# Idle matrix products in two pauses of the start, and the first tail's parts one step sooner, in an attention and ternary-FFN kernel on one core

## The chip, the core and the metric

The kernel runs on one core of one Trainium2 chip. The metric is device time in microseconds (us), the median of several runs of the whole kernel.

## What is computed

The input x has 8 batches of 1024 tokens with 256 features, all in f32. With `ln` for layer normalisation over the features:

```python
q, k, v = ln(x) @ Wq, ln(x) @ Wk, ln(x) @ Wv      # 16 query heads, 4 key/value heads, 16 wide
q, k = rope(q), rope(k)
o = softmax(q @ k.T / sqrt(256)) @ v               # each key head serves 4 query heads
x = x + ln(o @ Wo)
w = where(W > d, 1, where(W < -d, -1, 0)) * alpha  # d = 0.7 * mean(abs(W))
x = x + ln(ln(x) @ w.T + bias)
```

## The kernel before, in words

A **unit** is 512 tokens (half a batch); there are 16. A unit's attention has four **blocks** (one query head of each key group at a time), each block has 8 **steps** (key tiles of 128), and each step has four score tiles, so s counts score tiles from 0 to 2047 and step n ends at s = 4n + 4. One unit is 32 steps, 128 score tiles.

*Precision.* TensorE takes f32 operands as a high and a low part. `split_hi` (ACT, or POOL at L157) rounds a tile to its high part; `split_lo` (L162) subtracts that from the tile. `product` (L297, its matmuls recorded at L301) adds three products of the parts. So every projection needs both parts, turned by TensorE transposes (`transposed`, L262, matmuls at L267, copied out by ACT at L271).

*Project* (L323) makes a unit's q, k and v: normalise, split, `x` (the transposes), `q_product` (pq, L451), `kv` (pkv), `rotate_q` (L315 to L317), `rotate_k` (L400 to L406), `split_k`, `split_q`, and for the first unit `k` (ptk, L417) and `PickRows` (L531; pqs at L549, pk at L539), which places rows of q and k for the score products. *Tail* (L738) does what follows a unit's attention: `fetch`, `invert`, `scale` (the quotient), `attn` (pa, the product with Wo), `stats_a` (first norm and sum x1), `stats_x` (second norm, split), `x` (pt_ot), `ffn` (pf) and `stats_f` (last norm, sum, store). A tail works on two halves, 0 and 1, of its unit.

*The three products of attention.* `max_scores` (sm, L600) makes scores for the row maxima, which DVE reduces (mx, L612 and L625). `exp_one` (se, L673) makes them again, with the maximum taken off, for ACT's exponential (e, L694). `av_piece` (av, L714) multiplies by v.

*Order.* The kernel writes the order of PE, DVE, ACT and POOL by hand up to s = 8 (L1194), of PE, DVE and ACT behind that (L1250); POOL and the DMA queue of SP are then ordered when the kernel is compiled. The opening, in PE's order, is: eleven idle products (`keep_warm(11)`, L1197), the first unit's four groups of transposes (the loop at L1217: high and low part of its first half, then of its second), pq of half 0, pkv, the transposes ptv, pq of half 1, ptk, the picks, and the second unit's first transposes. Ten starting steps (-10 to -1) follow, in which DVE reduces four maxima each.

`keep_warm(n)` (L1002) issues n products of 128x512 of tiles that lie ready. They write a bank that nothing reads, so their only effect is TensorE's work.

From s = 0 the work goes in **windows** of 2 or 3 score tiles. Parts of projects and tails are entered in a list by step (`at`), step k of T_PARTS, T_FIRST, P_PARTS and the like counted from the unit's start. `collect` moves a step's parts to `ready`, and `do_parts` (L1127) takes them first in, first out. A part that needs a bank of PSUM (x, q, v, kv_and_dram, attn, ffn and others, `banked`, L1093) is taken in a window of two only, one to a window, and a part behind it waits. T_FIRST (L989) holds the steps of the first unit's tail, in the order of T_PARTS (L980), from step 32.

Of the kernel before, what the change touches and what calls it, by code (L numbers as in the profile page):

```python
# [28 lines left out]
def kernel(  # L29
# [120 lines left out]
    def fill_constant_parts(i):  # L150
        if i > 0:
            fill_rows(k_st[i], 1, NROW, 64 - NROW)
        nc.gpsimd.memset(v_aug[i], 1.0)
# [7 lines left out]
    def split_lo(eng, lo, src, hi):  # L161
        eng.tensor_tensor(lo, src, hi.bitcast(F32), ALU.subtract)  # L162
# [7 lines left out]
    def parts_of(w, name):  # L170
        return [const.tile(list(w.shape), F32R, name=name + l) for l in "hl"]

    def by_pairs(w):
        return w[:, :, :D].rearrange("p c (m e) -> p c e m", e=2)

    def by_place(w):
        return w[:, :, :D].rearrange("p c (e m) -> p c e m", e=2)
# [325 lines left out]
    def row_pickers():  # L503

        sel = q_st[1].rearrange("p j c t -> p (j c t)")[:, : 4 * G * P]
        nc.vector.memset(sel.bitcast(F32), 0.0)
        sel = sel.rearrange("p (l e j x) -> p l e j x", l=2, e=2, j=G)
        selk = tailp.tile([P, 2, P], F32R, tag="hl1", name="selk")
        nc.vector.memset(selk.bitcast(F32), 0.0)
        half = small.tile([P, P // 2], F32, tag="half", name="half", bufs=1)  # L510
        nc.vector.tensor_tensor(half, ident[:, : P // 2], ident[:, P // 2 :], ALU.add)
        eye = half.rearrange("p (a j d) -> p j a d", a=2, j=G)
        for e in range(2):
            for band, l in enumerate((0, 1, 0)):
                rows = sel[:, l, e].rearrange("p j (a b d e) -> p j a b d e", a=2, e=2, d=HD // 2)
                nc.vector.tensor_copy(rows[:, :, :, band, :, e], eye)
        eye = ident.rearrange("p (l r a d) -> p l r a d", l=2, r=2, a=2)
        for band, l in enumerate((0, 0, 1)):
            rows = selk.rearrange("p r (a b d) -> p r a b d", a=2, d=HD)
            nc.vector.tensor_copy(rows[:, :, :, band, :], eye[:, l])  # L520
        shift = const.tile([P, 1], F32, name="shift")
        rows = ident.rearrange("p (a d) -> p a d", a=2)[:, :, NROW:]
        nc.vector.tensor_reduce(shift, rows, AX.XY, ALU.add)
        nc.vector.tensor_scalar(shift, shift, -1.0, None, ALU.mult)
        low = const.tile([8 * UT, 1], F32, name="low")
        rows = ident[: 8 * UT, : 8 * UT].rearrange("p (a l x) -> p a l x", a=2, l=2)[:, :, 1]
        nc.vector.tensor_reduce(low, rows, AX.XY, ALU.add)
        nc.vector.tensor_scalar(low, low, -1.0, None, ALU.mult)
        return sel, selk, shift, low
# [421 lines left out]
    def part(of, u, name, *args):  # L951
        getattr(of[u], name)(*args)
# [11 lines left out]
    def load(u):  # L964
        x_sb[u] = load_x(u, "x", 2)
# [20 lines left out]


    P_SECOND = (26, 33, 34, 37, 43, 45, 49, 51, 52, 53, 55, 57)
    T_FIRST = (6, 8, 11, 12, 15, 17, 17, 18, 21, 24, 25, 26, 27, 28, 30, 32, 32, 34)  # L989
    P_FIRST = (47, 51, 52, 54, 57, 58, 59, 60, 62, 61, 63, 64)  # L990

    W_PARTS = (
# [9 lines left out]
    def keep_warm(n):  # L1002
        for _ in range(n):
            nc.tensor.matmul(warm[0], ident_r, sels[0][:, 0, 0], start=True, stop=True)

    x_parts = [("x", p, l) for p in range(2) for l in range(2)]
# [70 lines left out]
    for u in range(NU - 1):  # L1077
        start = SPU * (u + 1)
        at(start + 1, begin_tail, u)
        parts = T_PARTS if u < NU - 4 else W_PARTS  # L1080
        steps = {0: T_FIRST, NU - 2: T_LAST}.get(u, [k for k, *_ in parts])
        for k, (_, *p) in zip(steps, parts):
# [61 lines left out]
    def start_step(n):  # L1144
        for q in range(4):
            max_scores(maxima[0])
            maxima[0] += 1
            if q == 1:
                take_low()
        collect(n)  # L1150
        do_parts(99)
# [12 lines left out]
    def window(s):  # L1164


        late, size = s >= ends, window_size(s)
        if done:
            av_out(done.pop())
        if late:  # L1170
            for r2 in range(2):
                exp_two(s // 4, r2)
        else:
            end = min(maxima_by(s + size), 4 * NSTEP)
            for q in range(max(size, end - maxima[0])):
                if q < size:
                    exp_one(s + q)
                if maxima[0] < end:
                    max_scores(maxima[0])
                    maxima[0] += 1  # L1180
                if q == 0:
                    take_low()
            reduce_early(maxima[0])
        take_low()
        behind.append((s // (4 * NK), s, size))
        for n in range(s // 4, (s + size) // 4):
            collect(n)
        do_parts(3 - size if REGULAR <= s < ends else 99)
        av_windows(1 if late else 2)
        return s + size  # L1190
# [3 lines left out]
    with tc.manual_schedule(engines={E.PE, E.DVE, E.Activation, E.Pool}):  # L1194
        sels = row_pickers()
        warm.append(ps_av.tile([P, UQ], F32, tag="av", name="warm"))
        keep_warm(11)  # L1197
        p0 = projects[0] = Project(0, nc.vector)
        p1 = projects[1] = Project(1, nc.gpsimd)
        for p in range(2):  # L1200
            p0.stats(p)
        wqkv_s = parts_of(wqkv, "wqkv")
        nc.scalar.copy(by_place(wqkv_s[0]), by_pairs(wqkv))
        nc.scalar.copy(wqkv_s[0][:, :, D:], wqkv[:, :, D:])
        for p in range(2):
            p0.norm(p)
            p0.hi(p)
        for p in range(2):
            p0.lo(p)
        split_lo(nc.gpsimd, wqkv_s[1][:, :, D:], wqkv[:, :, D:], wqkv_s[0][:, :, D:])  # L1210
        split_lo(nc.gpsimd, by_place(wqkv_s[1]), by_pairs(wqkv), by_place(wqkv_s[0]))
        fill_constant_parts(0)
        for p in range(2):
            p1.stats(p)
        load(2)
        p2 = projects[2] = Project(2, nc.gpsimd)
        for p in x_parts:  # L1217
            part(projects, 0, *p)
        p0.q_product(0)
        p0.kv(0)  # L1220
        p0.kv(1)
        p0.rotate_q(0)
        p0.v()
        p1.norm(0)
        p1.hi(0)
        p1.lo(0)
        p1.norm(1)
        p0.q_product(1)
        p0.rotate_k()
        p0.split_k()  # L1230
        p0.split_q(0, (1,))
        p1.hi(1, nc.scalar)
        p0.rotate_q(1, nc.gpsimd)
        p0.k()
        spare[0] = 0
        picks.append(PickRows(sels))
        picks[0].q(0, 0, 0)
        p1.lo(1, nc.vector)
        picks[0].k(0, 0)
        picks[0].q(0, 1, 0)  # L1240
        picks[0].k(0, 1)
        p1.x(0, 0)
        p1.x(0, 1)
        p0.split_q(1, eng=nc.gpsimd, hi_eng=nc.scalar)
        for n in range(-START, 0):
            start_step(n)
        s = 0
        while s < 8:
            s = window(s)
# [76 lines left out]
```

## Time and profile before

| | us |
|---|---|
| three runs | 1627.93, 1629.83, 1637.51 |
| median | 1629.83 |
| the profiled execution, its time | 1631.22 |
| its span, first to last instruction | 1629.4 |
| PE busy | 1578.1 (97%) |
| DVE busy | 1398.3 (86%) |
| ACT busy | 1270.4 (78%) |
| POOL busy | 833.2 (51%) |
| mean granted clock of TensorE | 0.993 |

PE is TensorE's matrix products, PEld its weight loads, DVE the vector engine, ACT the scalar engine, POOL GpSimd, SP the engine whose queue issues all DMAs here. In a line of the timeline the columns are start, duration, engine, line of the code, operation, output and inputs, shape and count; what stands in brackets is the idle time just before it and what ended it. In a table of stretches each line is a stretch (from:to), its length, the busy time of the engine and its instructions in brackets, the granted clock (1.00 is full speed), the busy share of the DMA engines and the GB/s that they moved. Matmuls overlap, so a matmul's duration holds its way through the array; the distance from start to start tells what one costs in a row.

### The profile page before, as it was taken

To read this page: it belongs to the slowest core of one execution; us is meant where nothing else is said; L and a number is where in the kernel's file an instruction comes from. 1 tells how busy PE (TensorE), PEld (TensorE's weight loads), DVE (VectorE), ACT (ScalarE), POOL (GpSimd) and SP (SyncE) were. 2 spreads that over 40 slices of the span, in tenths; PEclk is the share of its full clock that TensorE was granted. 3 is DMA by queue.
4 is the path that set the end of the run, shared out by engine and by line. 5 is a ranking of instruction groups with operands and counts; after the bars stand their busy time and mean duration, and the time that the engine had idled before them with its cause. 6 is when DMAs were issued, how large, how long until landed. Compare 5 with 4: busy or idle time off the path is not lost.

```text
span 1629.4 us, 37176 instructions
## 1 busy us (share of the span) xinstructions
PE 1578.1 (97%) x14698; PEld 816.7 (50%) x14698; DVE 1398.3 (86%) x2050; ACT 1270.4 (78%) x2473; POOL 833.2 (51%) x1239
## 2 busy tenths in 40 slices
PE   7999999999999999999999999999999999999997
PEld 5544454554545545454544545455454554444444
DVE  7878888889898888989889898988989888999964
ACT  4667878788787887878788787887878787787784
POOL 5542357374654647455364845546474552333354
PEclk8999999999999999999999999999999999999999
DMA  4151516124141422514133161413314151131100
GB/s 140 53 83 49 106 53 113 62 67 112 57 108 47 88 71 60 125 47 104 61 79 80 57 128 38 103 56 82 80 57 97 47 105 46 43 74 34 42 15 27
DMA packets 86078, 117.98 MB, mean 72 GB/s; under 512 B 12088, under 2 KB 50808, under 8 KB 85752
## 3 DMA queue, kind: packets, MB, share of 16 engines
q1 hardware_dynamic: 85904, 115.60, 29.7%
q8 instruction: 116, 1.90, 0.5%
q14 instruction: 58, 0.48, 0.1%
HBM read 68.65 MB, written 45.88 MB: 70 GB/s over the span
## 4 chain that ended last, share of the span: by engine, by line
PE 81%; DVE 10%; POOL 3%; ACT 2%; issue 1%; DMA 1%; SPq 0%; POOLq 0%; ACTq 0%; DVEq 0%
PE av L714 29%; PE se L673 28%; PE sm L600 9%; DVE mx L625 8%; PE pa L301 3%; PE pq L301 3%; PE pf L301 2%; ACT e L694 2%; PE pt_xt L267 2%; PE pt_ot L267 1%; PE pkv L301 1%; PE pm L648 1%; DVE bnst L237 1%; POOL lnsc L242 0%; POOL xn L253 0%
## 5 line engine op out<-in xcount | busy, mean ns | idle before, releaser
L625 DVE TENSOR_REDUCE mx<-sm 128x2 f32<-128x1024 f32 (+1 forms) x1305 | 1205.1, 972 | 184.4 <-PE sm L600 164.7
L694 ACT ACTIVATE e<-se 128x512 f32<-128x512 f32 x1996 | 1056.9, 603 | 221.6 <-PE sm L600 176.2
L600 PE MATMUL sm<-k_st,q_st 64*128 64x512 f32 x2048 | 747.3, 449 | 7.9 <-DVE mx L625 4.6
L673 PE MATMUL se<-q_st,k_st 64*128 64x512 f32 x2048 | 705.9, 441 | 17.1 <-ACT e L694 14.6
L714 PE MATMUL av<-e,v_aug 128*32 128x256 f32 (+3 forms) x8600 | 605.7, 378 | 0.0
L673 PEld LDWEIGHTS se<-q_st,k_st 64*128 64x128 f32 x2048 | 325.1, 185 | 392.6 <-ACT e L694 303.6
L600 PEld LDWEIGHTS sm<-k_st,q_st 64*128 64x128 f32 x2048 | 325.7, 185 | 68.8 <-DVE mx L625 46.0
L714 PEld LDWEIGHTS av<-e,v_aug 128*32 128x32 f32 x8600 | 193.9, 109 | 213.0 <-issue 148.7
L241 POOL TENSOR_SCALAR lnsc<-mv 128x2 f32<-128x2 f32 (+1 forms) x134 | 25.6, 191 | 337.8 <-DVE mv L239 331.2
L788 POOL TENSOR_TENSOR xn<-xn,a 128x512 f32<-128x512 f32 x30 | 38.4, 1281 | 130.0 <-DMA a<-d_rec 104.5
L242 POOL TENSOR_TENSOR lnsc<-lnsc,mhalf 128x2 f32<-128x2 f32 (+1 forms) x134 | 92.2, 689 | 0.9
L157 POOL TENSOR_SCALAR xs<-xn 128x512 fp32r<-128x512 f32 x27 | 17.1, 634 | 128.3 <-DMA dq<-hlq 127.0
L162 POOL TENSOR_TENSOR hl<-xn,hl 128x512 fp32r<-128x512 f32 x54 | 68.7, 1284 | 0.1
L853 POOL TENSOR_TENSOR a<-a,bias_bc 128x512 f32<-128x512 f32 x30 | 38.4, 1280 | 53.7 <-ACT a L852 53.7
L253 POOL TENSOR_SCALAR xn<-x,lnsc 128x256 f32<-128x256 f32 x116 | 64.2, 560 | 2.3
L301 PE MATMUL pa<-woh,hl 128*128 128x256 f32 x240 | 46.2, 295 | 1.1 <-ACT e L694 1.1
L315 POOL TENSOR_TENSOR t<-q_rot,sin_q_sb 128x512 f32<-128x512 f32 x31 | 39.6, 1279 | 12.8 <-ACT q_rot L457 12.7
L237 DVE BATCH_NORM_STATS2 bnst<-x 128x6 f32<-128x256 f32 x124 | 45.9, 412 | 0.0
L301 PE MATMUL pq<-xt,wqkvh 128*128 128x256 f32 x256 | 45.0, 299 | 0.5 <-ACT e L694 0.5
L237 DVE BATCH_NORM_STATS2 bnst<-a 128x6 f32<-128x256 f32 x120 | 44.5, 413 | 0.1
L162 POOL TENSOR_TENSOR hlq<-q_rot,hlq 128x512 fp32r<-128x512 f32 x31 | 39.8, 1284 | 4.8 <-ACT hlq L159 4.5
L457 ACT COPY q_rot<-pq 128x512 f32<-128x512 f32 x32 | 18.7, 585 | 29.5 <-PE pq L301 29.5
(164 smaller groups left out, 1329.7 us busy)
## 6 DMA issues: line engine op xcount, KB each, us to landing
q_st<-dq SPq DMA_DIRECT2D x90, 256.0 KB
dq<-hlq SPq DMA_DIRECT2D x60, 256.0 KB
d_av<-avsb SPq DMA_DIRECT2D x60, 256.0 KB
x<-in_L_attn_x SPq DMA_DIRECT2D x15, 512.0 KB
xn<-d_av SPq DMA_DIRECT2D x30, 256.0 KB
a<-d_rec SPq DMA_DIRECT2D x30, 256.0 KB
xr<-in_L_attn_x SPq DMA_DIRECT2D x15, 512.0 KB
out_x<-a SPq DMA_DIRECT2D x30, 256.0 KB
```

The lines of the kernel that those rows point to most:

```text
L162: eng.tensor_tensor(lo, src, hi.bitcast(F32), ALU.subtract)
L237: nc.vector.bn_stats(st[:, t, :], src[:, t, :])
L242: nc.gpsimd.tensor_tensor(sc[:, 1, :], sc[:, 1, :], mhalf[:, :n], ALU.pow)
L253: eng.tensor_scalar(dst[:, t, :], src[:, t, :], sc[:, 0, t : t + 1] if eng is nc.gpsimd else mv[:, t, 0:1], sc[:, 1, t : t + 1], ALU.add i ...
L267: nc.tensor.transpose(pt[:, c, t * P : (t + 1) * P], src[:, t, c * P : (c + 1) * P], ident_r)
L301: nc.tensor.matmul(out, chunk(left[i], c), chunk(right[j], c), start=(k == 0), stop=(k == len(steps) - 1),)
L315: eng.tensor_tensor(dst, x, table.unsqueeze(1).to_broadcast(list(x.shape)), ALU.mult)
L600: scores = nc.tensor.matmul(sm[0][:, part, :], queries[rows], k_st[(u // UPB) % 3][rows, r2, ch * 512 : (ch + 1) * 512], start=True, stop= ...
L625: early[0] = nc.vector.tensor_reduce(mx[i][:, a, head_and_tile(i, r2, t), lo:n], sm[0][:, lo:n, :], AX.X, ALU.max).ins
L673: nc.tensor.matmul(sc if len(queries.shape) == 2 else sc.rearrange("p (j t) -> p j t", j=G), k_st[(i // G // UPB) % 3][rows, r2, kt * P : ...
L694: nc.scalar.activation(e, sc, AF.Exp, scale=1.0 / D**0.5)
L714: nc.tensor.matmul(av_ps[0][32 * r : 32 * r + 32, lo:hi], va[:, kt, r, :], es[i * NK + kt, r // 2, r % 2][:, lo:hi], start=(kt == 0 and lo ...
```

## The change

Ten idle products are put behind the first of the four groups of transposes of the first unit, ten more between `rotate_q` of its second half and `k`; on PE the second ten stand behind pq of half 1 and ahead of ptk. In T_FIRST, all entries from the fifth (`attn` of half 0) on are one step less; `fetch`, `invert` and the two `scale` stay.

```diff
-    T_FIRST = (6, 8, 11, 12, 15, 17, 17, 18, 21, 24, 25, 26, 27, 28, 30, 32, 32, 34)
+    T_FIRST = (6, 8, 11, 12, 14, 16, 16, 17, 20, 23, 24, 25, 26, 27, 29, 31, 31, 33)
...
         for p in x_parts:
             part(projects, 0, *p)
+            if p == x_parts[0]:
+                keep_warm(10)
         p0.q_product(0)
...
         p1.hi(1, nc.scalar)
         p0.rotate_q(1, nc.gpsimd)
+        keep_warm(10)
         p0.k()
```

## The prediction

> **What bounds the kernel now.** I read the page first, then the granted clock over stretches of the start, then the instructions of PE and DVE in order of time there, and last the first tail's stage (196 to 270 us). The page:
>
> ```profile
> span 1629.4 us, 37176 instructions
> PE 1578.1 (97%) x14698; PEld 816.7 (50%) x14698; DVE 1398.3 (86%) x2050; ACT 1270.4 (78%) x2473; POOL 833.2 (51%) x1239
> ...
> PE   7999999999999999999999999999999999999997
> ...
> PEclk8999999999999999999999999999999999999999
> ```
>
> PE is busy 97% of the span and carries 81% of the chain that ended last, so a microsecond saved ahead of the steady part reaches the end. Only the first and the last slice of PE are lower, and only the first slice of the clock is below 9. The change works in that first slice (0 to 41 us), and in the first tail. The next table is PE's busy time and clock (the column behind the count) in stretches cut where the clock changes:
>
> ```profile
> 10.68:14.07 3.39, 2.94 (x18) 0.50 0.91 270
> 14.07:17.46 3.39, 3.39 (x18) 0.50 1.08 241
> 17.46:20.87 3.41, 2.54 (x20) 1.00 0.80 222
> 20.87:24.34 3.47, 0.93 (x6) 1.00 0.53 153
> 24.34:27.73 3.39, 3.06 (x8) 0.50 0.00 0
> 27.73:31.13 3.40, 3.40 (x21) 0.50 0.02 5
> 102.95:106.30 3.35, 2.35 (x16) 0.99 0.60 109
> 7.27:10.68 3.41, 1.50 (x8) 1.00 1.01 348
> 106.30:109.65 3.35, 3.35 (x22) 0.50 0.01 3
> ```
>
> The clock moves in steps of some 3.4 us. It fell to 0.50 behind stretches with 1.50, 0.93 and 2.35 us of work, stayed at 1.00 behind one with 2.54 us, and came back only behind full ones (3.39, 3.40, 3.35). So between 2.35 and 2.54 us of work in 3.4 keep it up here, that is at most some 0.9 us of pause. Half speed lasts twice 6.8 us at the start.
>
> The two pauses and what ends them, PE first and then DVE:
>
> ```profile
> 8.33 0.54 PE L267 MATMUL pt_xt<-ident_r,xs 128*128 128x128 f32 x4
> 11.13 1.76 PE L267 MATMUL pt_xt<-ident_r,xs 128*128 128x128 f32 x12 [2.26 <-DVE xs L162]
> ...
> 20.28 0.40 PE L301 MATMUL pq<-xt,wqkvl 128*128 128x256 f32 x2
> 23.07 0.51 PE L417 MATMUL ptk<-ident_r,ks 128*128 128x128 f32 x4 [2.40 <-DVE ks L162]
> 23.51 0.49 PE L549 MATMUL pqs<-hlq,q_st 64*128 64x256 f32 x2
> 24.67 0.79 PE L549 MATMUL pqs<-hlq,q_st 64*128 64x256 f32 x2 [0.66 <-DVE hlq L162]
> ```
>
> ```profile
> 17.98 1.38 DVE L316 TENSOR_TENSOR q_rot<-q_rot,t 128x256 f32<-128x256 f32 x1
> ...
> 21.93 0.99 DVE L162 TENSOR_TENSOR ks<-k_rot,ks 128x256 fp32r<-128x256 f32 x1 [0.47 <-ACT ks L159]
> 22.85 1.76 DVE L162 TENSOR_TENSOR hlq<-q_rot,hlq 128x512 fp32r<-128x512 f32 x1
> ```
>
> Both pauses end on a DVE subtraction (L162). A third, shorter one, ahead of 24.67, ends on the next of them. PE cannot shorten these directly; it can only start DVE's inputs earlier.
>
> **First fill.** Ten products of 128x512 and ten weight loads are added on PE behind the first four transposes; nothing else is issued, no DMA, no work on ACT, DVE, POOL or SP. The product writes the bank that the eleven opening products use and reads two tiles long written, so it adds no wait. Duration: four such products at full clock end 0.99 us after they start (39.74 to the next at 40.73), so 0.25 each. 10 x 0.25 = 2.5 us from 8.73 (8.33 plus four loads, 0.40) to 11.2, against transposes that could start at 11.13: it costs 0.1. Queued behind it are those transposes alone; who waits for them is ACT's copies (L271). The clock is 1.00 at 8.73, so the cover is there. If it were not, the opening row gives 0.43 each (11 in 4.31 us, with a part already fast), and the fill costs 13.0 - 11.1 = 1.9 us.
>
> What it brings: the stretch 7.3 to 10.7 becomes full and the clock stays at 1.00 from 10.7 to 17.5. PE's 24 products of pq and pkv took 12.69 to 17.91, 5.2 us. At full clock the same twelve of pq took 19.00 to 20.68 less drain, 1.6 us, so 24 take 3.2. They start at about 12.5, since ACT's three copies of 0.53 us still pace them: pkv ends at 15.7 in place of 17.9, which is 2.1 us on PE.
>
> What is late next: DVE. Its rotation starts behind ACT's q_rot, at 14.8 in place of 16.24. It needs 0.69 + 0.98 + 0.41 + 0.41 us, to 17.35; the 1.38 of the row above was a 0.41 us operation beside POOL's subtraction of 17.49 to 19.07. That POOL work depends on the second x alone and does not move, so the operation that now lies beside it, t2k, is the one held, to about 19.2. Then the rest of t2k, 0.58 and 0.43 end at 20.55 where they ended at 21.46; ACT's hi part (0.40) and ks (0.99) follow, and the k transposes start at 22.15 in place of 23.07. **Gain 0.9 us.** Ends: 0.6 (POOL's rotation starts at 20.75 in place of 21.38, since its norm holds it, and may slow ks more) and 1.35 (no operation held). I take 0.9, by the L316 row.
>
> **Second fill.** Another ten, 2.5 us, now behind a q product that ends at 18.5: to 21.0. ptk is ready at 22.15, so they delay nothing while they take less than 0.36 us each; pauses of 1.1 us there and of 0.9 us ahead of hlq's low part (23.8) stay. Hidden work: price 0, up to 1.9 at 0.43 each if DVE were not late.
>
> Does the clock hold? In a stretch of 3.4 us that takes in both pauses PE has about 1.4 to 1.7 us of work, and in one with the first alone 2.3: below the 2.54 that kept it and at or below the 2.35 that did not. So the likelier case is that the clock falls near 24.3 again, and the 6.8 us at 0.50 stay. The work before 31.1 then runs as now, 0.9 us earlier, but 0.9 us more of it lies in the slow stretch, where at most half is lost; part of that is DVE's (2.36 us for each pair of maxima). I take 0.2 lost, ends 0 and 0.45.
>
> **The first tail.** No instruction is added; fourteen parts move. Walking the planner's lists with both sets of steps: the first attention product stays in the window at s = 190 (one projection product per window of two goes first), the second moves from 203 to 198, ahead of unit 4's kv, which moves from 201 to 200; the transposes move from 233, 238, 247, 252 to 230, 232, 244, 249, and the second ffn from 262 to 254. The window count stays 783. Its inputs: POOL had hl ready at 211.26, PE takes it at 219 or later, so no wait. x1's chain on POOL waited until 229.03 while POOL stood idle for 13.0 us; it starts some 4 us earlier, which relieves POOL's full run (8.00 of 8 us in 236 to 244). The first moved transpose ran at 251.76, its hl was done at 250.95: if POOL's order did not follow, PE would wait 2.3 - 0.8 = 1.5 us. On SP the d_k, k_rot and dk transfers of unit 4 go out 1.4 us later (its kv behind 1.62 us of products); these keys are first read from step 128 on, 77 steps later, so nothing waits. The last out transfer goes earlier. Upside: the unit of this tail took 98.9 us against 96.3 of the next, with PE idle 2.2 against 1.5, so 0.7 at most is idle time to be had. I take 0, ends -0.7 and +1.5.
>
> **Sum** against the profiled execution, 1631.22 us (span 1629.4 and 1.8 around it): 0.1 is inside the 0.9; -0.9 + 0.2 + 0 = -0.7, so 1630.5. The profiled execution stands 1.4 us above the median, 1629.83; on that footing 1629.1.
>
> **Rivals.** *The clock holds through 24 us* (the second fill works): from hlq's low part at 23.85, PE's back-to-back 4.29 us up to the first scores (24.67 to 28.96) halve to 2.15, and some 0.45 of waits on ACT's 0.69 us copies appear: scores at 26.45, 2.5 us earlier, and DVE's pairs half a microsecond more. -3.0: 1628.2, or 1626.8 by the median. For it: all pauses but two are gone. Against it: those two.
>
> *Slower: the fills run at half clock.* It decides from 0.25 us a product in the first pause. Were PE still slow at 8.73, the price is 1.9 us there, and 1.9 more if the second lot is slow too: 1635.0, or 1633.6. Against it: the transposes at 8.33 took 0.40 us for four loads, as the fast ones do; for it: where the clock's steps lie against the start may differ from run to run.
>
> *The tail's transposes wait for POOL*: +1.5 less 0.7, 1632.0, or 1630.6.
>
> *The change does nothing to the clock.* If pauses this short did not lower it, the fills lie in idle time and the time stays 1631.2, or 1629.8. The rows speak against it: 0.50 came behind each of the two pauses. The Trainium skill, "TensorE: Matmul & The Clock Gate", section "Why this matters for your kernels", asks only that no gap be longer than about 3 us; by that rule gaps of 2.26 and 2.40 us are harmless and filling them brings 0. The trace disagrees: 0.50 at 10.68 and 24.34.
>
> **How the numbers follow.** Chances: forecast 0.52, clock holds 0.27, no effect 0.07, slow fills 0.08, POOL wait 0.06. The forecast's own range has all its good ends, -1.35 - 0.7 = -2.05, and all its bad ones, -0.6 + 0.45 + 1.5 = +1.35: 1627.8 to 1631.2 by the median. The range reaches to the clock that holds, with 1.5 us for the scatter of a median (the three runs span 1627.93 to 1637.51): 1625.3; above it takes in the POOL wait and part of the slow fills: 1632.6. About 1% (16 us) is what a measurement of this kernel tells from no change; no case reaches it, so within 1% has 0.97, and 0.01 and 0.02 are left for faster and slower.
>
> **What would show it.** In the profile after: ten products in each pause, the first lot from 8.7 to 11.2; clock 1.00 from 10.7 to about 24; pkv ending near 15.7; ptk near 22.1; hlq's low part near 23.8; then 0.50 or 1.00 behind 24.3, which separates the forecast from its first rival; the second pa ahead of unit 4's pkv. Wrong if the clock is 0.50 in 11 to 17, if a fill takes over 0.3 us, or if pt_ot waits over 1 us for POOL.

## The result, and the profile after

| | us |
|---|---|
| changed kernel, median of 20 runs | 1625.38 (1622.57 to 1630.14) |
| before beside it, median of 20 runs | 1630.20 (1627.93 to 1640.26) |
| ratio | 0.9967, interval [0.9956, 0.9978] |
| profiled execution after, its time and span | 1627.03, 1625.2 |

The change gains 4.8 us by the medians, 0.3%. The forecast was 0.7 us: the direction was right, the size seven times too small, and the time lies at the edge of its range (1625.3). Three terms of the sum were mis-sized: the gain of the first fill (0.9 us), the fall of the clock behind the second (6.8 us at 0.50) and the first tail (0).

The page after, the lines that answer to those of before:

```profile
span 1625.2 us, 37184 instructions
PE 1576.5 (97%) x14702; PEld 813.9 (50%) x14702; DVE 1397.1 (86%) x2046; ACT 1270.1 (78%) x2473; POOL 833.8 (51%) x1239
...
PE   8999999999999999999999999999999999999997
...
PEclk9999999999999999999999999999999999999999
```

The first slice of the clock is now full. Twenty products came, but PE has only four more: sixteen pieces of av (8584 for 8600) went with the first tail's steps. PE's instructions in order of time, after:

```profile
8.70 2.56 PE L1004 MATMUL warm<-q_st,ident_r 128*128 128x512 f32 x10
11.16 1.22 PE L267 MATMUL pt_xt<-ident_r,xs 128*128 128x128 f32 x12
...
14.92 0.40 PE L301 MATMUL pkv<-xt,wqkvl 128*128 128x256 f32 x2
...
17.92 2.49 PE L1004 MATMUL warm<-q_st,ident_r 128*128 128x512 f32 x10
20.25 0.46 PE L417 MATMUL ptk<-ident_r,ks 128*128 128x128 f32 x4
20.64 0.50 PE L549 MATMUL pqs<-hlq,q_st 64*128 64x256 f32 x2
21.64 0.50 PE L549 MATMUL pqs<-hlq,q_st 64*128 64x256 f32 x2 [0.51 <-DVE hlq L162]
23.74 0.49 PE L539 MATMUL pk<-hlk,selk 128*128 128x512 f32 x1 [1.60 <-ACT hlk L423]
```

The first lot ends as forecast (11.2), pkv too (15.3 for 15.7). But ptk comes at 20.25, not 22.15. And a new pause stands ahead of pk: ACT's copy of ptk (hlk) stands in ACT's order behind an instruction that waits for POOL.

```profile
22.58 0.62 ACT L159 CAST xs<-xn 128x512 fp32r<-128x512 f32 x1 [3.15 <-POOL xn L253]
23.11 0.58 ACT L423 CAST hlk<-ptk 128x512 fp32r<-128x512 f32 x1
```

In this execution the clock fell behind that pause, at 25.1, for one stretch of 3.4 us. It fell once more from 103.6 to 107.0, near where the clock of before fell too (106.3 to 109.7):

```profile
18.24:21.65 3.41, 2.90 (x17) 1.00 0.92 225
21.65:25.06 3.41, 1.81 (x8) 1.00 0.29 71
25.06:28.46 3.40, 3.40 (x21) 0.50 0.27 92
```

**Where the time came from.** ACT's copy of a block's attention out of PSUM (avsb, L727) is one mark a block; 63 of the 64 blocks have one. After against before, in the two profiles:

| mark | before | after, earlier by |
|---|---|---|
| 0 to 3 | 95.90 to 176.63 | 2.56, 2.53, 2.54, 2.53 |
| 4, 5, 6, 7 | 198.32 to 273.09 | 2.50, 2.09, 0.66, 0.84 |
| 8 to 62 | 297.16 to 1587.75 | 3.18 at 8, 3.33 at 62 |

So 2.5 us come from the start and 0.7 from the first tail's stage; between the two ends nothing is given back. The last 0.9 us of the two executions' difference is not the change: before's clock fell once more in the last tail (1611 to 1615), which other executions of either kernel do or do not show.

A second profile of the changed kernel (`a_again` below) shows the other outcome: pk at 22.23, clock 1.00 to 1600 us, first mark 4.82 us ahead. At the next three it is 6.3 to 6.4 us ahead: the other 1.5 us are the fall near 105 us, which it lacks. That fall stands in four of the fourteen profiles, with and without the change, so it is not put down to the change.

Of the changed kernel's 25 runs, 12 had a mean clock of 0.999 or 1.000 and a median near 1623.75, 13 a lower one and 1626 to 1630. None of 107 runs of before beside the experiments reached 0.999. One stretch of 3.4 us at 0.50 takes 0.001 off the mean of such a run, so the mean tells how much was lost in all, not where; that the two groups differ at the start is shown by the two profiles alone.

### The profile page after: what moved, and what is told of

It reads as the page before. It is cut to its first block, busy times and chain, and to the rows that moved or that the text cites. A ratio compares the mean times of both kernels' runs of the same rounds, so it can differ in the third digit from the quotient of the medians.

```text
span 1625.2 us, 37184 instructions
## 1 busy us (share of the span) xinstructions
PE 1576.5 (97%) x14702; PEld 813.9 (50%) x14702; DVE 1397.1 (86%) x2046; ACT 1270.1 (78%) x2473; POOL 833.8 (51%) x1239
## 4 chain that ended last, share of the span: by engine, by line
PE 81%; DVE 10%; POOL 3%; ACT 2%; issue 2%; DMA 1%; SPq 0%; POOLq 0%; ACTq 0%; DVEq 0%
PE av L714 29%; PE se L673 28%; PE sm L600 9%; DVE mx L625 8%; PE pa L301 3%; PE pq L301 3%; PE pf L301 2%; ACT e L694 2%; PE pt_xt L267 2%; PE pt_ot L267 1%; PE pkv L301 1%; PE pm L648 1%; DVE bnst L237 1%; POOL lnsc L242 0%; DMA x<-in_L_attn_x 0%
## 5 line engine op out<-in xcount | busy, mean ns | idle before, releaser
L315 POOL TENSOR_TENSOR t<-q_rot,sin_q_sb 128x512 f32<-128x512 f32 x31 | 39.7, 1282 | 12.2 <-ACT q_rot L457 12.1
L301 PEld LDWEIGHTS pa<-woh,hl 128*128 128x128 f32 x240 | 34.6, 189 | 12.1 <-issue 6.3
```

The costliest lines, as they stand in the source:

```text
L301: nc.tensor.matmul(out, chunk(left[i], c), chunk(right[j], c), start=(k == 0), stop=(k == len(steps) - 1),)
L315: eng.tensor_tensor(dst, x, table.unsqueeze(1).to_broadcast(list(x.shape)), ALU.mult)
```

## The experiments

Theory: the products act through the clock alone, and the new steps of the first tail have an effect of their own. Rivals: only one of the two carries the gain; or the products act through order, layout or waits.

**The parts alone.** `e1_fills_only` is the change without its T_FIRST line, `e2_steps_only` that line alone, and the other two one lot each:

```diff
 # e3_first_lot
+            if p == x_parts[0]:
+                keep_warm(10)
 # e4_second_lot
         p0.rotate_q(1, nc.gpsimd)
+        keep_warm(10)
```

> Both lots of idle products, the first tail's old steps. Theory (the clock): the start is 2.5 us ahead of before's, as in the profile of the changed kernel (-2.53 us at each of the first four stores of a block), or some 4 us where the clock holds behind the second lot; by block 8 it is still 2.5 to 4 us, without the step to -3.2 us that the changed kernel shows there. Time 1626 to 1627, against 1630 of before. Rival (the first tail's steps carry the gain): within 1 us of before.

> The first tail's new steps, no idle products. By the profile pair the first tail's stage (blocks 4 to 8) gives 0.7 us: the stores of blocks 0 to 4 come as before, those from block 8 on 0.7 us earlier, and the time is 1629.5. My forecast was 0 for it, within -0.7 and +1.5. Rival: the steps gain only when the start is earlier, then the store of block 8 comes as before. As no product is added, this is also a second look at the start of before: the second x lands by 11.6 us again if its landing is fixed, later if it differs from run to run.

> Only the first ten products. Theory: the clock stays at 1.00 from 10.7 to 20 us, pkv ends near 15.3, ptk comes 1 to 2.8 us earlier; the pause ahead of ptk stays at 2.3 us or more, so the clock falls behind it, and the 6.8 us at 0.50 stay: some 1.5 to 2.5 us gained, 1628. Rival (the lots help only together): under 0.5 us, since DVE, not PE, ends the second pause.

> Only the second ten products. Theory: the clock falls at 10.7 as before and ptk stays near 23.1; behind it the pause of 0.7 us alone is left, so the clock holds from 24.3 to 31.1 in most runs: the first scores come 1.5 to 2 us earlier, 1628. Rival (the pauses left behind ptk are enough to lower the clock): 0.50 behind 24.3 as before, time as before within 0.5 us.

| kernel | median us (before 1630.25) | ratio, interval |
|---|---|---|
| both lots | 1626.31 | 0.9981 [0.9973, 0.9989] |
| steps | 1629.34 | 0.9996 [0.9988, 1.0005] |
| first lot | 1628.87 | 1.0002 [0.9988, 1.0015] |
| second lot | 1629.42 | 0.9996 [0.9988, 1.0005] |

The lots carry most of it, and need each other: both give 3.9 us by the medians (1.8 to 4.4 by the interval), each alone can't be told from before. With the first lot alone ptk comes as early (20.89), but PE has idled 2.82 us ahead of it, and the clock falls for three stretches, 21.5 to 31.8:

```profile
18.12:21.53 3.41, 0.64 (x5) 1.00 0.74 195
21.53:24.94 3.41, 3.41 (x11) 0.50 0.54 156
24.94:28.35 3.41, 3.41 (x22) 0.50 0.02 5
28.35:31.75 3.40, 3.40 (x15) 0.50 0.00 0
```

With the second alone DVE is as late as before (ptk 22.90), so its ten products leave 1.20 us ahead of ptk and 0.65 behind, both in the stretch 21.4 to 24.8, and the clock falls at 24.8 as in before. The first lot makes DVE early enough for the second to reach ptk. In e1's profile the marks are further ahead than expected, 4.81 us at the first and 6.35 at mark 3: the clock holds there up to 1600 us, at the start as well as near 105. The steps alone gain 0.9 us by the medians, which the noise does not separate from nothing; what they do is shown below by the blocks.

In e2's profile no product stands in the first pause, and yet the clock held through 10 to 23 us. There the eleven opening products ran slow to their end (5.03 us, 4.31 in before), the pause began later (1.72 us idle), and the clock came up to 1.00 only at 9.8, inside the pause, where it came up at 7.3 in before. So the fall behind this pause is not certain: it hangs on where the 3.4 us steps meet it. And the second x landed at 13.1 us there, by 11.6 in before's profile, although no instruction ahead of it differs.

**The clock or the order.** The same products, 16 columns wide in place of 512; and half the number:

```diff
 # e7_narrow
+                warm[0][:, :16], ident_r, sels[0][:, 0, 0, 0, :16], start=True, stop=True
 # e8_half_lots
-        keep_warm(10)
+        keep_warm(5)
```

> The changed kernel with the twenty idle products 16 columns wide in place of 512: same count, places, order and waits, next to no work. Theory (the products act through the clock): the pauses stay at over 1.5 us, the clock falls in them, time as with the first tail's steps alone, 1629.3. Rival (they act through the order or the code's layout): 1625.4 as the changed kernel.

> The changed kernel with five products in each lot. Theory: pauses of 1.2 us and more are left in both places; by the rows (held at 2.54 us of work in 3.4, fell at 2.35) that is at the edge, so the clock falls in part of the runs: 1627 to 1629, more scatter than the changed kernel. Rival (any work in the pause is enough): 1625.4.

Narrow: 1631.22 us beside 1630.62 of before, ratio 1.0002 [0.9988, 1.0017]; the clock falls at 12.1 and 22.3. The same instructions in the same places without their work bring nothing, so order and layout are out. Ahead of 12.1 the profile has only 0.87 us of pause, and 2.54 us of busy time in the 3.41 of the stretch, since ten narrow products take 1.25 us there; the clock fell even so. Half: 1626.38, 0.9969 [0.9955, 0.9982], better than forecast; 4 of 11 runs at a clock of 0.999. In its profile the clock held behind the first pause (1.06 us idle) and behind the one ahead of ptk (1.20), and fell at 24.6, behind a third one of 1.35 us ahead of pk.

**The third pause.** Six more products where PE waited for hlk, or ACT's order changed so that it does not wait:

```diff
 # e5_third_lot
         picks[0].q(0, 0, 0)
+        keep_warm(6)
         p1.lo(1, nc.vector)
 # e6_hi_behind_k
-        p1.hi(1, nc.scalar)
         p0.rotate_q(1, nc.gpsimd)
         keep_warm(10)
         p0.k()
+        p1.hi(1, nc.scalar)
```

> The changed kernel with six more idle products ahead of the first pk, where its profile shows PE waiting 1.60 us for ACT's hlk. Theory (the clock): the fall at 25 us goes, and with it the slower half of the runs; nearly all are then where the changed kernel's faster half is: 1624 against 1625.4. Where hlk is early, the six cost up to 1.5 us at the start and give nothing back. Rival (that pause does not set the clock, the steps of the clock do by chance): still two groups of runs, median as the changed kernel or 1 us above.

> The changed kernel with ACT's high part of the second unit's second half put behind its copy of ptk, no product more. That copy no longer waits for POOL's norm when the second x lands late (13 us in place of 11.6). Theory (an order on ACT, behind the landing of x, makes the third pause): pk comes 0.3 us behind hlq's low part in every run, the clock holds through 25 us, 1624. Rival: DVE's low part of the same half, which stands between the two copies of q and needs ACT's high part, is late in its place; then the pause only moves to the second pk, time as the changed kernel.

Third lot: 1624.98 (before 1630.62), 0.9965 [0.9951, 0.9979]; 11 of 12 runs lie in 1623.9 to 1626.4 where the changed kernel's 20 lie in 1622.6 to 1630.1, so the times lie closer together, but for one of 1632.65. The cost is some 1.2 us at the first scores (25.64; 24.42 in `a_again`), and the median can't be told from the changed kernel's. ACT's order: 1624.06, 0.9976 [0.9954, 0.9998], four of seven runs at 0.999, two far off (1631.07, 1635.81); as expected in its middle, not in its scatter. Its profile holds the clock through the start, with pk at 22.16, but x landed at 11.8 there; `e10_both` below, where x landed at 12.8, shows a fall with this order too.

**The first tail.** In each of the profiles with the new steps, e9 and e10 below apart, the table of PE's waits has a line that none with the old ones has; here the changed kernel's, columns us in total, times, longest:

```profile
PE se L673 <- DMA q_st<-ml: 1.3, 1, 1.3
```

The ml transfer brings a block's row maxima into the q operand; ks, dk and k_st are unit 4's keys, written to DRAM (dk) and read back. On SP's queue (start, duration, what), before and then the changed kernel:

```profile
240.43 1.13 SPq L448 DMA_DIRECT2D dk<-ks  x2
241.67 1.40 SPq L664 DMA_DIRECT2D q_st<-ml  x2
243.69 0.80 SPq L499 DMA_DIRECT2D k_st<-dk  x2
```

```profile
234.91 3.01 SPq L448 DMA_DIRECT2D dk<-ks  x4
238.18 3.60 SPq L499 DMA_DIRECT2D k_st<-dk  x6
241.87 1.40 SPq L664 DMA_DIRECT2D q_st<-ml  x2
```

In before two dk went ahead of ml and the other eight transfers behind it. With stats_a sooner POOL starts the low part of unit 4's keys sooner (236.1, before 242.9), and all ten of their transfers pass ml. Three kernels on it: the changed one again; unit 4's `kt` (the part that makes and stores its keys) two steps later with its stores behind ml; that with e6's order.

```diff
 # e9_keys_later, e10_both
-    P_SECOND = (26, 33, 34, 37, 43, 45, 49, 51, 52, 53, 55, 57)
+    P_SECOND = (26, 33, 34, 37, 43, 45, 49, 51, 54, 53, 55, 57)
...
+            behind = [behind_latest] if u == 4 and p[0] == "kt" else behind
```

> The changed kernel as it is, on the chip and beside the runs of the next two. Expected: 1625.4, in two groups (clock 0.999 and near 1623.7; clock 0.997 and near 1627.3); a wait of 0.9 to 1.3 us of PE for the transfer of ml in the second block of the first tail's stage, as in all six profiles with the new steps.

> The changed kernel with unit 4's kt two steps later and its stores behind the latest ml transfer, so that SP issues ml ahead of dk and k_st. Theory (the new steps bring a wait of their own on SP's queue, worth 0.9 to 1.3 us): the wait is gone, blocks 5 to 7 of the first tail's stage take 73.9 us in place of 75.0 (76.2 with the old steps), the time falls by 1.1 us against the changed kernel run beside it. Rival (the wait is slack, DVE's maxima or POOL is late next): under 0.4 us.

> The last one with ACT's high part behind its copy of ptk as well. If both theories hold, the clock falls at the start in few runs and the ml wait is gone: 1623 against 1625.4 of the changed kernel and 1630.3 of before. Rival: the third pause was rare in this set of runs, then no better than the kernel with the later keys alone.

And the early half of the steps alone:

```diff
 # e12_first_half
-    T_FIRST = (6, 8, 11, 12, 14, 16, 16, 17, 20, 23, 24, 25, 26, 27, 29, 31, 31, 33)
+    T_FIRST = (6, 8, 11, 12, 14, 16, 16, 17, 20, 24, 25, 26, 27, 28, 30, 32, 32, 34)
```

> The changed kernel, but of the first tail only attn, stats_a and the first stats_x are a step sooner; the second stats_x, the transposes, both ffn and stats_f stand at before's steps. It tells which moved parts bring the gain of 1.3 us in blocks 5 to 7 (76.2 to 76.3 us with the old steps, 74.7 to 75.1 with the new) and which the wait for ml. Theory: the wait comes with the early half, since POOL gets to unit 4's keys sooner and their stores pass ml on SP; the gain comes with the late half, whose transposes and ffn meet other windows: then blocks 5 to 7 take 77 us or more, with a wait of some 1 us for ml. Rival: the early half brings both, by unloading POOL: then 75 us here as well.

Blocks 5, 6, 7 and their sum, mark to mark, with PE's busy time. Before:

```profile
220.93:248.38 27.45, 26.93 (x263) 1.00 0.16 47
248.38:273.09 24.71, 23.93 (x235) 1.00 0.54 120
273.09:297.16 24.07, 23.20 (x227) 1.00 0.60 109
220.93:297.16 76.23, 74.06 (x721) 1.00 0.42 90
```

Changed kernel:

```profile
218.84:247.72 28.88, 27.16 (x257) 1.00 0.24 74
247.72:272.25 24.53, 24.04 (x245) 1.00 0.44 92
272.25:293.98 21.73, 21.21 (x213) 1.00 0.60 115
218.84:293.98 75.14, 72.41 (x707) 1.00 0.41 92
```

The early half alone (e12), then keys later (e9), the sums:

```profile
215.51:292.74 77.23, 74.08 (x713) 1.00 0.39 89
```

```profile
218.97:292.75 73.78, 72.33 (x707) 1.00 0.42 94
```

The sums hardly differ between runs: 76.23 to 76.26 in the four profiles with the old steps, 74.74 to 75.14 in the seven with all new ones. Block 4 is left out, since it took 22.6 to 23.5 us with the old steps and 22.6 to 23.1 with the new. So the early half costs 1.0 us, its ml wait (1.1 in e12); the late half gains 2.1 to 2.5; with ml ahead on SP (issued at 236.91) the wait is gone and the sum is 73.8, as forecast.

The late half's gain is PE's busy time, 74.08 to 72.41. From before to the changed kernel the single groups nearly keep theirs (av 28.63 and 28.62, se 33.74 and 33.68, sm 35.87 and 35.41), but sm and se, which overlap, cover 38.27 us together before and 36.48 after, worked out from the traces' rows (38.2 to 38.3 in every profile without the moved late half, e12 among them, 36.5 to 36.6 in every one with it). So more of sm lies beside se, by 1.79 us, which covers the 1.65 us of busy time. Why the moved parts bring that about was not tried; av has fewer pieces (432 and 416) in the same time.

Times, beside 1630.83 of before: changed kernel 1625.65 (5 runs), keys later 1624.60 (12), both 1623.25 (12), the lowest median. The keys bring 1.05 us by the medians where the profile has 1.1. The ratios to before, [0.9953, 0.9977], [0.9950, 0.9976] and [0.9953, 0.9980], do not separate the three; the blocks do. In e10's profile the clock fell at 25.3 even so, with pauses of 0.41, 0.27 and 0.37 us only, and again from 104 to 124 us. e12 took 1627.20 beside 1631.26, [0.9961, 1.0002].

## Why the prediction was wrong, point by point

The step that failed is the first fill's gain, 0.9 us with ends of 0.6 and 1.35: the k transposes came 2.2 to 2.8 us sooner, and the first four marks 2.5 us sooner in the profile in which the clock still fell. Two more terms went the same way, the 6.8 us at 0.50 behind the second fill (3.4 us in one profile, none in the other) and the first tail's 0 (1.1 to 1.5 us over blocks 5 to 7).

*What bounds the kernel* held: a microsecond at the start reached the end (2.53 at mark 3; marks 8 to 62 stay within 0.2 of each other).

*The first fill* held on PE: 0.256 us a product, 2.56 in all, no delay beyond 0.03, pkv at 15.3.

*"What is late next: DVE"* failed, in the sentence that POOL's work "depends on the second x alone and does not move". It moved: DVE's rotation came earlier and lay beside POOL's norm, which took longer. The fills-only profile has x as early as before (11.64). POOL in before, then POOL and DVE in that profile:

```profile
15.16 1.09 POOL L253 TENSOR_SCALAR xn<-x,lnsc 128x256 f32<-128x256 f32 x2
...
17.49 1.58 POOL L162 TENSOR_TENSOR xs<-xn,xs 128x512 fp32r<-128x512 f32 x1
```

```profile
15.28 2.01 POOL L253 TENSOR_SCALAR xn<-x,lnsc 128x256 f32<-128x256 f32 x2
...
18.20 1.34 POOL L162 TENSOR_TENSOR xs<-xn,xs 128x512 fp32r<-128x512 f32 x1
```

```profile
17.11 0.53 DVE L400 TENSOR_TENSOR t2k<-k_rot,sin_k_sb 128x128 f32<-128x128 f32 x2 [0.16 <-ACT k_rot L387]
...
18.42 1.40 DVE L406 TENSOR_TENSOR k_rot<-k_rot,t2k 128x256 f32<-128x256 f32 x1
20.29 0.43 DVE L162 TENSOR_TENSOR ks<-k_rot,ks 128x256 fp32r<-128x256 f32 x1 [0.47 <-ACT ks L159]
```

The norm took 2.01 for 1.09, so the subtraction came at 18.20 for 17.49, and t2k ran free (0.53) ahead of it. One operation was held for about a microsecond, as I had it, but the last of the three (k_rot, 1.40), and ks ran in 0.43 for 0.99. ptk: 20.9, a gain of 2.2 against the 0.9 of the sum; 2.8 where x lands late, as in the changed kernel's profile. I moved one engine's work and left its neighbour's where it stood. That the norm was slow because of the rotation beside it is read from the times, not tried by itself.

*The second fill* held in its length, 2.49 us. But ptk's pause shrank to nothing or 0.5 us where I left 1.1 of it, and in the changed kernel's first profile the fill itself held ptk for some 0.2 us: ks ended at 19.88 and ptk started at 20.25, against 20.72 and 20.87 in the fills-only profile.

*"Does the clock hold?"* fell on that, and on the threshold. The likelier case had it fall for 6.8 us; in two profiles of the changed kernel it fell once for 3.4 us and held once, and the mean clock of the 25 runs suggests that about half held. The rival's price was too low as well: -3.0 forecast, 4.82 at the first mark, from ptk's 2.2 and from the first scores at 24.42 where I had 26.45. The cut between 2.35 and 2.54 us of work in 3.4 is no rule either: it fell behind 2.77 (e10) and 2.54 (e7), and held behind 2.13 (e2):

```profile
21.89:25.30 3.41, 2.77 (x18) 1.00 0.30 105
```

```profile
9.85:13.26 3.41, 2.13 (x21) 1.00 1.03 353
```

The first holds products of 64 rows (pqs), two pk and transposes, the second projections and transposes. Busy time in the profile is not what the clock goes by; what is, stays open. Nor does one full stretch always bring it back: in e10 PE was busy for the whole of six in a row, 104 to 124 us, before the clock rose.

*The first tail* was taken as 0, "0.7 at most is idle time to be had". The order on PE came as forecast (the second pa at 219.15, unit 4's pkv at 222.22). But the parts do not only fill idle time: they change how PE's work lies together, and busy time fell by 1.65. Its wait I sought on POOL; it came on SP, a queue for which I wrote "nothing waits" after asking only who waits for the keys, not what stands behind their ten transfers.

*The rivals.* Clock holds: in about half of the runs, as far as the mean clock tells, and worth more than priced. Slow fills: not seen in the changed kernel's two profiles, where each lot ran at 0.25 us a product. The tail's transposes waiting for POOL: not seen. No effect on the clock: out, by the narrow products. The Trainium skill's rule there ("TensorE: Matmul & The Clock Gate", "Why this matters for your kernels": no gap above about 3 us) does not suffice here: the clock fell behind pauses of 1.20 and 0.65 us in one stretch (e4), behind one of 1.35 us (e8) and behind shorter ones (e7, e10).

## What to carry to other kernels

Before a pause is costed, ask what the engine that ends it runs beside: here, where work was moved beside another engine's, that engine became slower as well, and the next collision moved with it. Where the clock falls in pauses, two fills can be worth more than the sum of each (3.9 us by the medians; 1.4 and 0.8 alone, neither clear of the noise), since a pause that is left lowers the clock for what follows. And when parts are moved on a queue, list what stands behind their transfers, not only who waits for them.

## What the runs showed that was not expected

The landing of the second x lay anywhere from 11.6 to 13.1 us, for one and the same kernel too (12.96 and by 11.64 in the changed kernel's two profiles). The third pause went with it: where x had landed by 11.64 (`a_again`, fills only) PE did not wait for hlk, at 12.43 (e9) and 12.96 (changed kernel) it waited 1.37 and 1.60 us; e12, at 12.31, did not wait, with ptk half a microsecond later. Some runs hold the clock at 0.50 for long: from 104 to 124 us in e10's profile (1635.36 us, mean clock 0.990). Single times near 1637 have a mean clock as low, 0.988 to 0.990, in runs of before as well; none of those was profiled, so that they hold such a stretch is not shown.
